# An attention loop on TensorE: small products and VectorE's side work take other places in the order

## The chip, the cores and the metric

The kernel runs on one core of one Trainium2 chip. A core has five engines that run their own instruction streams: TensorE (PE, matrix products; its weight loads are shown as PEld), VectorE (DVE), ScalarE (ACT), GpSimd (POOL) and SyncE (SP, used here for DMA queues and marks). The metric is the device time of one execution in microseconds (us), lower is better. A kernel is run several times and the median is given. A profile is one more execution, with its own time.

## What is computed

There are B = 16 graphs' inputs x of N = 1024 nodes and C = 64 channels, and one N x N matrix adj. All is in 32-bit floats. Layer 0 is an attention whose softmax goes over axis 1 and whose result passes through adj; layer 1 adds a two-hop graph convolution with adj. Each layer is followed by a residual sum and a layer norm.

```python
Q = jnp.einsum('bnc,oc->bno', x, Wq) + bq
K = jnp.einsum('bnc,oc->bno', x, Wk) + bk
V = jnp.einsum('bnc,oc->bno', x, Wv)
score = jnp.einsum('bnc,bmc->bnm', Q, K)
score = jax.nn.softmax(score, axis=1)
score = jnp.einsum('bnm,mc->bnc', score, adj)
x = _layernorm(x + jnp.einsum('bnm,bmc->bnc', score, V))
...
x_stack = [x0]
for support in (adj, adj):
    x1 = jnp.einsum('ij,bjk->bik', support, x0)
    x_stack += [x1, 2.0 * jnp.einsum('ij,bjk->bik', support, x1) - x0]
x = _layernorm(x + concatenate(x_stack) @ weight + bias)
```

## The kernel before

The kernel reorders the attention: it computes y = adj x for all batches first (so score times adj never exists as an N x N product), and then per batch the softmaxed scores times y, and that times Wv. Products with adj are done by a seven-product scheme over the four quadrants of adj ("hops": `hop_0` and `hop_1` make adj x for batches 0 to 7 and 8 to 15, `hop_z` starts layer 1). Each of the seven products of a hop has a number n; product n needs a sum of quadrants on the adj side (`sums_of_adj`) and one on the other side (`Hop.sums`), made by VectorE.

Batches go in pairs: p = 0 to 7 is the pair, j = 0 or 1 the batch in it. Batch j's channels lie on partitions 0-63 (j = 0) or 64-127 (j = 1). Nearly every product of the attention loop has a 64x64 stationary tile, so the array is used as four quarters: the row half is set by the partitions that are read, the column half by the partitions that are written. "Upper" below is the row half of partitions 0-63, "lower" that of 64-127. A product in 32-bit floats is two matmul instructions on the chip.

The loop runs over steps (p, m), m = 0 to 7 being a block of 128 of the softmax rows. One step makes the scores of the next block, `nxt`, and uses up the exponentials of this one. In TensorE's order a step is, with the row half in brackets:

1. `scores(sc, nxt, 0, h)` for h = 0, 1 [upper], with the end of the last step's run between them (`tail.part(1, 1)` [lower])
2. `weighted(before, 1, h)` [lower]: us times the exponentials of the last block, second half, accumulated into `acc`
3. the first part of a run, `todo[0].part(0, 0)` [upper]. A run is a 128 x 256 piece of one hop product; 69 of them are taken one or two a step from the list `runs`
4. `scores(sc1, nxt, 1, 0)` [lower]; then, in some steps, the small product of j = 0 [upper]; then `scores(sc1, nxt, 1, 1)` [lower], `todo[0].part(0, 1)` [upper]
5. `weighted(p, m, 0, 0)` [upper], the small product of j = 1 [lower], `weighted(p, m, 0, 1)` [upper], `todo[-1].part(1, 0)` [lower]

The small products are: `values` of pair p-1 in step (p, 1) (16 products of 64 columns per batch), `project` of pair p+1 in step (p, 4) (2 of 512 columns per batch, makes `GT`), and `mix` of an earlier pair in steps (p, 7), (p, 0), (p, 2), (p, 3) (4 of 192 columns per batch). Both of a step, j = 0 and then j = 1, are written into the same PSUM bank, the one of two (`f0`, `f1`) that the step's run doesn't use, so the second waits until the first is evicted. Each has an eviction for ScalarE (`by_scalar`) and one for VectorE (`by_vector`).

The softmax of a block is `exps` (line 384 on): VectorE takes the negated maximum of a row (`nm`, L393), ScalarE the exponential with its row sum (`e`, L395). `sc` and `sc1` are two PSUM tiles of two banks each, so the scores of one block can start only when the exponential of the last has read its tile. In the next step `scaled` makes `ri` = 1/sum (L402) and `us` = y times `ri` (L404), without which `weighted` cannot start.

VectorE's stream in a step is: eviction of the last step's run, `ri`, `us`, first maximum, `by_vector` of the first small product, what `first_gap` holds for this step, second maximum, `by_vector` of the second small product, (with two runs) the eviction of the first run, what `second_gap` holds. The two dictionaries are filled by `at(...)` by hand: hop sums, weight preparation (`value_weights`, `mix_weights`), and for each pair `means`, `centre`, `spread`, `normed`, and the transposes (`transposed`, `x0T`), which VectorE does blockwise and POOL's DMA queue finishes by way of DRAM (one write, four reads). `attended` copies `acc` to `oT` on ScalarE at m = 0; it must be read before the next pair's `weighted` can open `acc` again. SP's queue in the loop carries only marks that keep products of the two row halves into one bank in order. The order of each engine's stream is the order of the program (`manual_schedule`).

Of the kernel before, what the change touches and what calls it, by code (L numbers as in the profile page):

```python
# [9 lines left out]
FP = mybir.dt.float32  # L10
# [16 lines left out]
def gnn_kernel(  # L27
# [13 lines left out]
    nc = tc.nc  # L41
# [112 lines left out]
    def mix_weights():  # L154
        nc.vector.tensor_add(w24, w1s[:, 2], w1s[:, 4])
        nc.vector.tensor_scalar(w3[:, 0], w24, 2.0, None, op0=ALU.mult)
        nc.vector.tensor_add(w3[:, 1], w1s[:, 1], w1s[:, 3])
        nc.vector.tensor_sub(w3[:, 2], w1s[:, 0], w24)
        for j in range(2):
            nc.vector.tensor_add(w3[half[j], 2], w3[half[j], 2], ident[half[j], half[j]])  # L160
        centred(w3)

# [178 lines left out]
    def project(p, js, pq):  # L341


        if 0 in js:
            GT[p] = att.tile([P, N], FP, tag="GT", name="GT")
        for b in range(2):
            for j, t in zip(js, pq):
                nc.tensor.matmul(  # L348
                    t[half[b]], g2[half[j], half[j]], xT(p)[half[j], ts(b, H)], start=True, stop=True
                )  # L350

        def places():
            for j, t in zip(js, pq):
                for b in range(2):
                    g = by_block(GT[p])[half[j], 2 * b : 2 * b + 2]
                    yield j, g, t[half[b]].rearrange("c (a k n) -> c a k n", a=2, k=K8), gb[half[b]]

        def by_scalar():
            for j, g, q, bias_ in places():
                if j == 0:  # L360
                    nc.scalar.activation(g, q, AF.Identity, bias=bias_)  # L361

        def by_vector():
            for j, g, q, bias_ in places():
                if j == 1:
                    nc.vector.tensor_scalar(g, q, bias_, None, op0=ALU.add)
        return by_scalar, by_vector

    def means(p):
        XM[p] = small.tile([P, G], FP, tag="xm", name="xm", bufs=NP)  # L370
        nc.vector.tensor_reduce(XM[p], rows(p), AX.X, ALU.add)
        nc.vector.tensor_scalar(XM[p], XM[p], 1.0 / C, None, op0=ALU.mult)

    def centre(p):
        nc.vector.tensor_tensor(
            rows(p), rows(p), XM[p][:, :, None].to_broadcast([P, G, C]), ALU.subtract
        )
# [48 lines left out]

    def attended(p):
        OT[p] = att.tile([P, N], FP, tag="oT", name="oT", bufs=1)
        nc.scalar.activation(by_block(OT[p]), by_place(ACC.pop(p)), AF.Copy)

    def values(p, js, po):


        for k in range(K8):
            for t in range(2):
                for j, o in zip(js, po):
                    n = k * P + t * C
                    nc.tensor.matmul(  # L438
                        o[half[t], ts(k, C)], OT[p][half[j], n : n + C], wv2[half[j], half[j]],
                        start=True, stop=True,  # L440
                    )

        def by_vector():
            for j, o in zip(js, po):
                r = xs[:, p, :, half[j]]
                nc.vector.tensor_add(r, o.rearrange("p (k c) -> p k c", c=C), r)
        return (lambda: None), by_vector

# [31 lines left out]
    def mix(p, kk, js, pm):  # L480


        pm = [t.rearrange("p (s k c) -> p s k c", s=4, k=2) for t in pm]
        for k in range(2):
            for c in range(2):
                for j, t in zip(js, pm):
                    n = (kk + k) * P + c * C
                    nc.tensor.matmul(  # L488
                        t[half[c], 0:3, k], X0T[p][half[j], n : n + C], w3[half[j]],
                        start=True, stop=True,  # L490
                    )

# [8 lines left out]
        def by_vector():  # L501
            for j, t in zip(js, pm):
# [3 lines left out]
                )  # L506
        return by_scalar, by_vector

    def both(what, *args, banks=None):

        return what(*args, (0, 1), banks or [f_tile(f"both{j}") for j in range(2)])

# [71 lines left out]
    for hop, orders in (  # L584
        (hop_0, (((6, 7), ONE), ((5, 3), ONE))),
        (hop_1, (((1, 2), ONE), ((6, 7, 4), ONE), ((5, 3), ONE))),
        (hop_z, (((1, 2), ONE), ((3,), ONE), ((5,), ONE), ((6, 7, 4), ONE))),
    ):
        runs += [(hop, n, g) for order, groups in orders for g in groups for n in order]
# [9 lines left out]
    at(first_gap, (0, 2), sums_of_adj, 4)  # L599
    at(second_gap, (0, 3), value_weights)  # L600
    at(second_gap, (0, 5), mix_weights)
    for step, n in ((1, 0), 1), ((1, 1), 2), ((1, 6), 4), ((2, 1), 3):
        at(second_gap, step, hop_1.sums, n)
    for step, n in ((HP + 1, 1), 1), ((HP + 2, 0), 2), ((HP + 2, 1), 3), ((HP + 2, 5), 4):
        at(second_gap, step, hop_z.sums, n)
    for p in range(NP):
        at(second_gap, (p, 5 if p != HP + 2 else 6), means, p)
        if p in (HP + 1, NP - 1):
            at(second_gap, (p, 6), centre, p)
        else:  # L610
            at(first_gap, (p + 1, 0), centre, p)
        if p + 1 < NP:
            at(second_gap, (p + 1, 2), spread, p)
            at(second_gap, (p + 1, 3), normed, p)
            at(first_gap, (p + 1, 4), x0T, p)
        if p + 2 < NP:
            at(second_gap, (p, 7), lambda p: transposed(p, xT(p)), p + 2)

# [45 lines left out]
    for p in range(NP):  # L664
        q = p - 1
        for m in range(K8):
# [9 lines left out]
            if before:  # L676
                weighted(*before, 1, 0)
            scaled(p, m)
            for evict in late:
# [5 lines left out]
            if before:  # L685
                weighted(*before, 1, 1)
                if m == 0:
                    attended(q)
                PU.pop(before)
            todo[0].part(0, 0)  # L690
            what = small_of.get((p, m))
            sc1 = sc_tile("sc1")
            scores(sc1, *nxt, 1, 0)
            if what:
                by_scalar, by_vector = what[0](*what[1:], (0,), [f_other("small0")])
                by_scalar()
            else:
                todo[0].part(0, 1)
# [37 lines left out]
    for h in range(2):  # L736
        for j in range(2):
# [4 lines left out]
            if sum_mark:  # L742
                behind_mark([made], sum_mark.pop())
    attended(NP - 1)
    evict()
# [417 lines left out]
```

## Time and profile before

| what | us |
|---|---|
| median of 3 runs (lowest to highest) | 582.25 (582.12 to 582.33) |
| the profiled execution, device time | 582.28 |
| its span in the profile | 580.5 |
| PE busy | 565.7 (97%) |
| PEld busy | 405.8 (70%) |
| DVE busy | 442.5 (76%) |
| ACT busy | 244.6 (42%) |
| POOL busy | 153.0 (26%) |
| first maximum of step (0,0) to that of step (7,6) | 37.67 to 417.88 |

Times of the trace are counted from the span's start; 1.8 us of the device time lie around the span. A line of a timeline gives the start, how long the piece took, engine, source line, operation, out<-in, partitions x elements and the count of merged instructions, and in brackets how long the engine had been idle and what released it. A group's line gives its count, busy time, the mean of one in ns, and the idle time ahead of it. A busy PE means that at least one matmul is under way; the four quarters of the array are not told apart. The clock granted to TensorE was 0.994 of full speed over the span.

### The profile page before, as it was taken

How to read it: one execution, taken by the hardware profiler on the slowest of the kernel's cores; microseconds unless marked ns; L12 is line 12 of the kernel's file. 1: busy time of each engine (PE TensorE's matmuls, PEld its weight loads, DVE VectorE, ACT ScalarE, POOL GpSimd, SP SyncE). 2: the span in 40 equal slices, each digit the busy share in tenths (PEclk: the TensorE clock that was granted, in tenths of full speed). 3: DMA queues.
4: the chain of work that ended last, by engine and by line, in shares of the span. 5: the costliest groups of instructions: out<-in, count | busy, mean ns of one | idle time of the engine just before them, and what ended most of it. 6: DMA issues, size and time to landing. Idle time of an engine off the chain costs nothing.

```text
span 580.5 us, 14496 instructions
## 1 busy us (share of the span) xinstructions
PE 565.7 (97%) x6150; PEld 405.8 (70%) x6150; DVE 442.5 (76%) x725; ACT 244.6 (42%) x517; POOL 153.0 (26%) x145
## 2 busy tenths in 40 slices
PE   9999999999999999999999999999999999999992
PEld 8757647567756766766676776677668789888652
DVE  0789788878877788787788778888847475799784
ACT  1133544545456455553554455455431300041561
POOL 0001001211211120121121012102102795693784
PEclk9999999999999999999999999999999999999997
DMA  8902002012022020101202010100201400001943
GB/s 262 333 5 71 2 2 75 37 38 76 1 73 74 3 73 23 53 37 39 75 1 75 14 62 32 44 2 2 75 1 43 103 1 2 1 17 44 204 144 100
DMA packets 20994, 33.66 MB, mean 58 GB/s; under 512 B 3010, under 2 KB 12482, under 8 KB 20546
## 3 DMA queue, kind: packets, MB, share of 16 engines
q0 software_dynamic: 6880, 18.88, 11.2%
q1 hardware_dynamic: 14050, 13.86, 7.3%
q8 instruction: 48, 0.79, 0.6%
q14 instruction: 16, 0.13, 0.1%
HBM read 16.48 MB, written 12.06 MB: 49 GB/s over the span
## 4 chain that ended last, share of the span: by engine, by line
PE 91%; DVE 3%; ACT 2%; issue 2%; DMA 0%; POOL 0%; SPq 0%; POOLq 0%; ACTq 0%; DVEq 0%
PE p L267 21%; PE sc L382 18%; PE acc L416 17%; PE w L770 15%; PE w L1078 3%; PE small L488 3%; PE small L348 3%; PE pu L257 3%; PE wide L770 2%; PE small L438 2%; PE pv L257 1%; PE p L257 1%; PE both L488 1%; ACT GT L361 1%; DVE nm L393 1%
## 5 line engine op out<-in xcount | busy, mean ns | idle before, releaser
L382 PE MATMUL sc<-xT,GT 64*64 64x512 f32 x1024 | 242.1, 592 | 0.7 <-ACT e L395 0.5
L416 PE MATMUL acc<-e,us 64*64 64x512 f32 x1008 | 242.0, 592 | 0.2 <-DVE us L404 0.2
L395 ACT ACTIVATE e<-sc,nm 128x1024 f32<-128x1024 f32 x128 | 142.7, 1115 | 118.2 <-DVE nm L393 117.9
L393 DVE TENSOR_REDUCE nm<-sc 128x1 f32<-128x1024 f32 x128 | 156.0, 1220 | 22.2 <-PE sc L382 21.2
L456 POOL TENSOR_TENSOR rstd<-var,expo 128x16 f32<-128x16 f32 (+3 forms) x21 | 50.9, 2428 | 145.4 <-DVE var L454 145.3
L416 PEld LDWEIGHTS acc<-e,us 64*64 64x64 f32 x1008 | 69.8, 133 | 27.4 <-issue 12.3
L382 PEld LDWEIGHTS sc<-xT,GT 64*64 64x64 f32 x1024 | 69.4, 132 | 13.3 <-issue 6.2
L334 POOL DMA_DIRECT2D d<-blocks x14 | 8.4, 596 | 200.2 <-DVE blocks L329 200.2
L267 PE MATMUL p<-XB,S 64*64 64x256 f32 x480 | 59.2, 378 | 0.0
L267 PE MATMUL p<-UY,aT 64*64 64x256 f32 x480 | 59.0, 377 | 0.0
L267 PE MATMUL p<-UY,S 64*64 64x256 f32 x384 | 46.2, 376 | 0.0
L267 PE MATMUL p<-XB,aT 64*64 64x256 f32 x352 | 42.8, 377 | 0.0
L267 PEld LDWEIGHTS p<-XB,S 64*64 64x64 f32 x480 | 33.7, 133 | 12.7 <-issue 4.5
L267 PEld LDWEIGHTS p<-UY,aT 64*64 64x64 f32 x480 | 33.9, 133 | 11.5 <-issue 2.8
L488 PE MATMUL small<-w,x0T_k 64*64 64x192 f32 x384 | 40.7, 329 | 0.0
L488 PEld LDWEIGHTS small<-w,x0T_k 64*64 64x64 f32 x384 | 25.1, 132 | 14.3 <-DVE xs L503 11.3
L267 PEld LDWEIGHTS p<-UY,S 64*64 64x64 f32 x384 | 27.1, 133 | 9.8 <-issue 2.9
L498 ACT ACTIVATE UY<-small 128x128 f32<-128x128 f32 x48 | 13.3, 277 | 46.5 <-PE small L488 46.5
L267 PE MATMUL p<-xs,aT 64*64 64x256 f32 x256 | 31.5, 377 | 0.0
L267 PEld LDWEIGHTS p<-XB,aT 64*64 64x64 f32 x352 | 24.8, 133 | 9.5 <-issue 3.3
L267 PE MATMUL p<-xs,S 64*64 64x256 f32 x256 | 30.9, 376 | 0.0
L503 DVE TENSOR_TENSOR xs<-small,bias 128x128 f32<-128x128 f32 x48 | 14.0, 291 | 22.0 <-ACT XB L499 21.9
(211 smaller groups left out, 941.0 us busy)
## 6 DMA issues: line engine op xcount, KB each, us to landing
d<-blocks POOLq DMA_DIRECT2D x14, 512.0 KB, 2.9
xs<-own POOLq DMA_DIRECT2D x8, 512.0 KB, 6.5
xT<-d POOLq DMA_DIRECT2D x28, 128.0 KB, 3.3
x0T<-d POOLq DMA_DIRECT2D x28, 128.0 KB, 2.9
out_dram<-xs SPq DMA_DIRECT2D x14, 256.0 KB, 2.2
xs<-in_x_dram SPq DMA_DIRECT2D x3, 1024.0 KB, 7.2
aT<-in_adjT_dram SPq DMA_DIRECT2D x8, 256.0 KB, 5.2
aT<-in_adjT_dram SPq DMA_DIRECT2D x4, 512.0 KB, 8.2
```

The costliest lines, as they stand in the source:

```text
L257: nc.tensor.matmul(po[t * w : (t + 1) * w], SIDE[n][:, k, j : j + w], self.side[n][:, :, k, :], start=start, stop=True, skip_group_check=True,
L267: nc.tensor.matmul(po[half[c]], SIDE[n][half[t], k, i * P + c * C : i * P + (c + 1) * C], self.side[n][half[t], :, k, :], start=t == 0 and ...
L348: nc.tensor.matmul(t[half[b]], g2[half[j], half[j]], xT(p)[half[j], ts(b, H)], start=True, stop=True)
L382: nc.tensor.matmul(sc[half[c], ts(h, H)], GT[p][half[j], m * P + c * C : m * P + (c + 1) * C], xT(p)[half[j], ts(h, H)], start=True, stop= ...
L393: nc.vector.tensor_reduce(nm, sc, AX.X, ALU.max, negate=True)
L395: nc.scalar.activation(e, sc, AF.Exp, bias=nm, accum_out=sm[:, j : j + 1])
L416: nc.tensor.matmul(ACC[p][half[j], ts(h, H)], us[half[t], j], es[j][half[t], ts(h, H)], start=m == 0 and t == 0, stop=m == K8 - 1, skip_gr ...
L456: nc.gpsimd.tensor_tensor(rstd, var, expo[:, 0:n], ALU.pow)
L488: nc.tensor.matmul(t[half[c], 0:3, k], X0T[p][half[j], n : n + C], w3[half[j]], start=True, stop=True,)
L503: nc.vector.tensor_tensor(xs[:, p, kk : kk + 2, half[j]], t[:, 2], bias[:, None, :].to_broadcast([P, 2, C]), ALU.add,)
L770: nc.tensor.matmul(po[:, ts(g, b.shape[1] * P)], a[:, k, ts(g, P)], b[:, :, k, :], start=start and g == 0 and k == 0, stop=True, skip_grou ...
L1078: nc.tensor.matmul(po, SIDE[n][:, k, ts(i, P)], B_F[n][:, k, cols], start=k == 0, stop=k == K4 - 1)
```

## The change

The change leaves what is computed as it is and alters the order.

- Small products come as a list of parts (`made`), issued apart from their evictions. The first part of j = 0 is issued ahead of `scores(sc1, nxt, 1, 0)` and the other parts behind it; of j = 1, the first part where the product was, the others behind `weighted(p, m, 0, 1)`. Only `values` has two parts; `project` and `mix` have one.
- `project`'s evictions are split otherwise: of j = 0 one half goes to ScalarE and one to VectorE; of j = 1 both go to ScalarE. Before, ScalarE had both of j = 0 and VectorE both of j = 1.
- All entries of `second_gap` but the first transpose move to `first_gap`, many to another step; `mix_weights` loses its last operation, which becomes an entry of step (1, 0). `means` no longer scales by 1/C; `centre` does that in one `scalar_tensor_tensor`.
- `exps(nxt, 1, sc1)` stands behind the first run's eviction in steps with two runs.
- `attended` is done in two halves, the first behind `weighted(before, 1, 0)`.
- In the hops' orders, products 6, 7 and 4 (of `hop_1` and `hop_z`) run one after the other instead of interleaved, and the sums that they need are made later.

```diff
--- before.py
+++ after.py
@@ -158,7 +158,6 @@
         nc.vector.tensor_sub(w3[:, 2], w1s[:, 0], w24)
         for j in range(2):
             nc.vector.tensor_add(w3[half[j], 2], w3[half[j], 2], ident[half[j], half[j]])
-        centred(w3)
@@ -343,37 +342,43 @@
         if 0 in js:
             GT[p] = att.tile([P, N], FP, tag="GT", name="GT")
-        for b in range(2):
-            for j, t in zip(js, pq):
-                nc.tensor.matmul(
-                    t[half[b]], g2[half[j], half[j]], xT(p)[half[j], ts(b, H)], start=True, stop=True
-                )
-        def places():
+        def made():
+            for b in range(2):
+                for j, t in zip(js, pq):
+                    nc.tensor.matmul(
+                        t[half[b]], g2[half[j], half[j]], xT(p)[half[j], ts(b, H)],
+                        start=True, stop=True,
+                    )
+        def places(vector):
             for j, t in zip(js, pq):
                 for b in range(2):
-                    g = by_block(GT[p])[half[j], 2 * b : 2 * b + 2]
-                    yield j, g, t[half[b]].rearrange("c (a k n) -> c a k n", a=2, k=K8), gb[half[b]]
+                    if vector == ((j, b) == (0, 1) if len(js) == 1 else j == 1):
+                        g = by_block(GT[p])[half[j], 2 * b : 2 * b + 2]
+                        q = t[half[b]].rearrange("c (a k n) -> c a k n", a=2, k=K8)
+                        yield g, q, gb[half[b]]
         def by_scalar():
-            for j, g, q, bias_ in places():
-                if j == 0:
-                    nc.scalar.activation(g, q, AF.Identity, bias=bias_)
+            for g, q, bias_ in places(False):
+                nc.scalar.activation(g, q, AF.Identity, bias=bias_)
         def by_vector():
-            for j, g, q, bias_ in places():
-                if j == 1:
-                    nc.vector.tensor_scalar(g, q, bias_, None, op0=ALU.add)
-        return by_scalar, by_vector
+            for g, q, bias_ in places(True):
+                nc.vector.tensor_scalar(g, q, bias_, None, op0=ALU.add)
+        return (made,), by_scalar, by_vector
     def means(p):
         XM[p] = small.tile([P, G], FP, tag="xm", name="xm", bufs=NP)
         nc.vector.tensor_reduce(XM[p], rows(p), AX.X, ALU.add)
-        nc.vector.tensor_scalar(XM[p], XM[p], 1.0 / C, None, op0=ALU.mult)
     def centre(p):
-        nc.vector.tensor_tensor(
-            rows(p), rows(p), XM[p][:, :, None].to_broadcast([P, G, C]), ALU.subtract
+        nc.vector.scalar_tensor_tensor(
+            rows(p), XM[p][:, :, None].to_broadcast([P, G, C]), -1.0 / C, rows(p),
+            op0=ALU.mult, op1=ALU.add,
         )
     def scores(sc, p, m, j, h):
@@ -424,27 +429,32 @@
         if h == 1 and not (t and m == K8 - 1):
             sum_mark.append(passed(made))
-    def attended(p):
-        OT[p] = att.tile([P, N], FP, tag="oT", name="oT", bufs=1)
-        nc.scalar.activation(by_block(OT[p]), by_place(ACC.pop(p)), AF.Copy)
+    def attended(p, h):
+        if h == 0:
+            OT[p] = att.tile([P, N], FP, tag="oT", name="oT", bufs=1)
+        a = slice(2 * h, 2 * h + 2)
+        nc.scalar.activation(by_block(OT[p])[:, a], by_place(ACC[p])[:, a], AF.Copy)
     def values(p, js, po):
-        for k in range(K8):
-            for t in range(2):
-                for j, o in zip(js, po):
-                    n = k * P + t * C
-                    nc.tensor.matmul(
-                        o[half[t], ts(k, C)], OT[p][half[j], n : n + C], wv2[half[j], half[j]],
-                        start=True, stop=True,
-                    )
+        def made(ks):
+            for k in ks:
+                for t in range(2):
+                    for j, o in zip(js, po):
+                        n = k * P + t * C
+                        nc.tensor.matmul(
+                            o[half[t], ts(k, C)], OT[p][half[j], n : n + C], wv2[half[j], half[j]],
+                            start=True, stop=True,
+                        )
         def by_vector():
             for j, o in zip(js, po):
                 r = xs[:, p, :, half[j]]
                 nc.vector.tensor_add(r, o.rearrange("p (k c) -> p k c", c=C), r)
-        return (lambda: None), by_vector
+        parts = [lambda b=b: made(range(4 * b, 4 * b + 4)) for b in range(2)]
+        return parts, (lambda: None), by_vector
     def inv_std(sq, n):
@@ -481,14 +491,16 @@
-        for k in range(2):
-            for c in range(2):
...
+        def made():
+            for k in range(2):
+                for c in range(2):
...
@@ -504,11 +516,14 @@
                     xs[:, p, kk : kk + 2, half[j]], t[:, 2],
                     bias[:, None, :].to_broadcast([P, 2, C]), ALU.add,
                 )
-        return by_scalar, by_vector
+        return (made,), by_scalar, by_vector
     def both(what, *args, banks=None):
-        return what(*args, (0, 1), banks or [f_tile(f"both{j}") for j in range(2)])
+        parts, *evict = what(*args, (0, 1), banks or [f_tile(f"both{j}") for j in range(2)])
+        for do in parts:
+            do()
+        return tuple(evict)
     u = att.tile([P, K4, Q], FP, tag="u", name="u", bufs=1)
@@ -583,8 +598,8 @@
     runs = []
     for hop, orders in (
         (hop_0, (((6, 7), ONE), ((5, 3), ONE))),
-        (hop_1, (((1, 2), ONE), ((6, 7, 4), ONE), ((5, 3), ONE))),
-        (hop_z, (((1, 2), ONE), ((3,), ONE), ((5,), ONE), ((6, 7, 4), ONE))),
+        (hop_1, (((1, 2), ONE), ((6,), ONE), ((7,), ONE), ((4,), ONE), ((5, 3), ONE))),
+        (hop_z, (((1, 2), ONE), ((3,), ONE), ((5,), ONE), ((6,), ONE), ((7,), ONE), ((4,), ONE))),
     ):
         runs += [(hop, n, g) for order, groups in orders for g in groups for n in order]
     two_runs = {(0, 1), (0, 2), (1, 0), (HP, 5), (HP + 1, 5), (HP + 1, 6)}
@@ -597,24 +612,23 @@
     at(second_gap, (0, 0), lambda: transposed(1, xT(1)))
     at(first_gap, (0, 1), sums_of_adj, 1)
     at(first_gap, (0, 2), sums_of_adj, 4)
-    at(second_gap, (0, 3), value_weights)
-    at(second_gap, (0, 5), mix_weights)
-    for step, n in ((1, 0), 1), ((1, 1), 2), ((1, 6), 4), ((2, 1), 3):
-        at(second_gap, step, hop_1.sums, n)
-    for step, n in ((HP + 1, 1), 1), ((HP + 2, 0), 2), ((HP + 2, 1), 3), ((HP + 2, 5), 4):
-        at(second_gap, step, hop_z.sums, n)
+    at(first_gap, (0, 3), mix_weights)
+    at(first_gap, (0, 4), value_weights)
+    for step, n in ((1, 0), 1), ((2, 0), 2), ((2, 5), 3), ((3, 0), 4):
+        at(first_gap, step, hop_1.sums, n)
+    at(first_gap, (1, 0), centred, w3)
+    for step, n in ((HP + 1, 5), 1), ((HP + 2, 0), 2), ((HP + 2, 7), 3), ((NP - 1, 0), 4):
+        at(first_gap, step, hop_z.sums, n)
     for p in range(NP):
-        at(second_gap, (p, 5 if p != HP + 2 else 6), means, p)
-        if p in (HP + 1, NP - 1):
-            at(second_gap, (p, 6), centre, p)
-        else:
-            at(first_gap, (p + 1, 0), centre, p)
+        at(first_gap, {2: (2, 1), 6: (4, 5)}.get(p, (p, 5)), means, p)
+        at(first_gap, {6: (5, 6)}.get(p, (p, 6)), centre, p)
         if p + 1 < NP:
-            at(second_gap, (p + 1, 2), spread, p)
-            at(second_gap, (p + 1, 3), normed, p)
+            at(first_gap, (p + 1, 2), spread, p)
+            at(first_gap, (p + 1, 3), normed, p)
             at(first_gap, (p + 1, 4), x0T, p)
         if p + 2 < NP:
-            at(second_gap, (p, 7), lambda p: transposed(p, xT(p)), p + 2)
+            at(first_gap, (p, 7), lambda p: transposed(p, xT(p)), p + 2)
     small_of = {(p, 1): (values, p - 1) for p in range(1, NP)}
     small_of.update({(p, 4): (project, p + 1) for p in range(NP - 1)})
@@ -675,6 +689,8 @@
             scores(sc, *nxt, 0, 1)
             if before:
                 weighted(*before, 1, 0)
+                if m == 0:
+                    attended(q, 0)
             scaled(p, m)
             for evict in late:
                 evict()
@@ -685,14 +701,18 @@
             if before:
                 weighted(*before, 1, 1)
                 if m == 0:
-                    attended(q)
+                    attended(q, 1)
                 PU.pop(before)
             todo[0].part(0, 0)
             what = small_of.get((p, m))
             sc1 = sc_tile("sc1")
+            if what:
+                parts, by_scalar, by_vector = what[0](*what[1:], (0,), [f_other("small0")])
+                parts[0]()
             scores(sc1, *nxt, 1, 0)
             if what:
-                by_scalar, by_vector = what[0](*what[1:], (0,), [f_other("small0")])
+                for do in parts[1:]:
+                    do()
                 by_scalar()
             else:
                 todo[0].part(0, 1)
@@ -712,15 +732,19 @@
                 todo[0].part(1, 0)
             weighted(p, m, 0, 0)
             if what:
-                by_scalar, by_vector = what[0](*what[1:], (1,), [f_other("small1")])
+                parts, by_scalar, by_vector = what[0](*what[1:], (1,), [f_other("small1")])
+                parts[0]()
                 by_scalar()
-            exps(*nxt, 1, sc1)
-            if what:
-                by_vector()
             if len(todo) > 1:
                 todo[0].part(1, 1)
                 todo[0].evict()
             weighted(p, m, 0, 1)
+            if what:
+                for do in parts[1:]:
+                    do()
+            exps(*nxt, 1, sc1)
+            if what:
+                by_vector()
             todo[-1].part(1, 0)
             for do in second_gap.get((p, m), ()):
                 do()
@@ -741,7 +765,8 @@
             )
             if sum_mark:
                 behind_mark([made], sum_mark.pop())
-    attended(NP - 1)
+    for h in range(2):
+        attended(NP - 1, h)
     evict()
     assert not runs
```

More of the change, by code (lines that the diff above doesn't have):

```diff
@@ L483, in mix @@
         pm = [t.rearrange("p (s k c) -> p s k c", s=4, k=2) for t in pm]
-        for k in range(2):
-            for c in range(2):
[L486 to L491, printed above, removed]
+        def made():
+            for k in range(2):
+                for c in range(2):
+                    for j, t in zip(js, pm):
+                        n = (kk + k) * P + c * C
+                        nc.tensor.matmul(
+                            t[half[c], 0:3, k], X0T[p][half[j], n : n + C], w3[half[j]],
+                            start=True, stop=True,
+                        )
         def part(dst, j):
```

## The prediction

> **What bounds the kernel now.** I read the page first, for the chain that ended last and the busy times.
>
> ```profile
> PE 91%; DVE 3%; ACT 2%; issue 2%; DMA 0%; POOL 0%; SPq 0%; POOLq 0%; ACTq 0%; DVEq 0%
> ...
> L393 DVE TENSOR_REDUCE nm<-sc 128x1 f32<-128x1024 f32 x128 | 156.0, 1220 | 22.2 <-PE sc L382 21.2
> ```
>
> TensorE is the bound, and VectorE has slack: 22.2 us of its idle time lies ahead of the maxima, waiting for scores. But TensorE's busy time hides its own loss. Every product here has a 64x64 stationary tile, so four fit in the array; a "busy" TensorE may have a half of it empty. So I took the matmuls of the attention loop by form, from the first maximum of step (0,0), 37.67 us, to that of step (7,6), 417.88 us.
>
> ```profile
> L416 PE MATMUL acc<-e,us 64*64 64x512 f32 x992 | 238.2, 592 | 0.2 <-DVE us L404 0.2
> L382 PE MATMUL sc<-xT,GT 64*64 64x512 f32 x996 | 237.5, 592 | 0.7 <-ACT e L395 0.5
> L488 PE MATMUL small<-w,x0T_k 64*64 64x192 f32 x384 | 40.7, 329 | 0.0
> L438 PE MATMUL small<-wv,oT 64*64 64x64 f32 x448 | 19.7, 222 | 0.1
> L348 PE MATMUL small<-xT,g 64*64 64x512 f32 x56 | 14.9, 604 | 1.7 <-ACT GT L361 1.7
> ```
>
> The timeline shows what one occupies: 512-column products of one row half start every 0.43 us (scores at 153.15, 153.58, 154.01, 154.44), those with 256 columns every 0.215, with 192 every 0.16, with 64 every 0.058. So the loop holds 2044 x 0.43 + 2192 x 0.215 (the products of L267) + 384 x 0.16 + 448 x 0.058 = 1438 us for one quarter of the array, 359 us for all four. The stretch lasts 380.2. About 21 us of it is an array partly empty: the ceiling of any reordering. A step without small product fills 12 slots of 0.43 = 5.16 us; with mix 5.80, with project 6.02, with values 6.09, with two runs 6.88.
>
> Then where it is empty, from timelines of one step per kind. Step (3,4), project:
>
> ```profile
> 207.48 0.62 PE L348 MATMUL small<-xT,g 64*64 64x512 f32 x2
> ...
> 208.08 0.59 PE L382 MATMUL sc<-xT,GT 64*64 64x512 f32 x2
> ...
> 208.94 0.60 PE L382 MATMUL sc<-xT,GT 64*64 64x512 f32 x2
> 209.21 0.62 PE L416 MATMUL acc<-e,us 64*64 64x512 f32 x2
> 210.19 0.65 PE L348 MATMUL small<-xT,g 64*64 64x512 f32 x2 [0.36 <-ACT GT L361]
> ```
> ```profile
> 208.76 1.38 ACT L361 ACTIVATE GT<-small,gb 64x512 f32<-64x512 f32 x2 [2.76 <-PE small L348]
> 210.16 1.11 ACT L395 ACTIVATE e<-sc,nm 128x1024 f32<-128x1024 f32 x1
> ```
>
> The first small product is through at 208.10, yet its eviction starts at 208.76, just after the scores that precede it in program order (208.08 + 0.59 = 208.67). The second small product uses the same bank and waits for both evictions, to 210.19. The lower row half is empty from 209.37, the upper from 209.64: (0.82 + 0.56)/2 = 0.69 us. The exponential behind the evictions is late too, and the next scores wait for it (0.32 us of one half, 0.16). Together 0.85.
>
> Step (3,1), values:
>
> ```profile
> 188.37 0.57 PE L438 MATMUL small<-wv,oT 64*64 64x64 f32 x14
> ...
> 189.21 0.60 PE L382 MATMUL sc<-xT,GT 64*64 64x512 f32 x2
> 189.22 0.88 PE L438 MATMUL small<-wv,oT 64*64 64x64 f32 x7
> 189.85 0.65 PE L382 MATMUL sc<-xT,GT 64*64 64x512 f32 x2
> ```
>
> Sixteen of the 32 small instructions run at full rate ahead of the scores they follow in program order; the rest limps, and stops for 0.43 us. Upper half: done at 188.32 + 16 x 0.058 = 189.25 if unbroken, next product at 189.88, 0.63 lost; lower half: 189.64 to 189.85, 0.21. Mean 0.42; the second small product costs 0.09 (bank) and 0.12 (the acc behind it at 191.91, due 191.68). Together 0.63.
>
> A mix step, (2,3): scores end 154.87, second small product at 155.11, once the bank is evicted: 0.24 of one half, 0.12; in steps (p,0), where the copy of acc comes first, (0.29 + 0.15)/2 = 0.22. Steps (0,5), (0,6): seven small VectorE operations and a mean between the second maximum and the next `ri`, 1.0 and 1.1 us.
>
> Sum: project 7 x 0.85 less 0.5 for the first two = 5.5; values 7 x 0.63 = 4.4; mix 18 x 0.12 + 6 x 0.22 = 3.5; pair 0 2.1; the other 5.5 is scattered.
>
> [...]
>
> **The change, part by part.**
>
> *Small product j=0 ahead of scores (1,0).* Same matmuls, same row halves in the same order, so no TensorE work is added. Its end is signalled before the scores': project eviction at 208.19 for 208.76. Half now goes to VectorE (0.75; its first maximum ends about 208.1), so both are done by 208.95 instead of 210.15, before the lower half is free (209.37): the 0.69 goes, and the exponential starts about 1.1 us earlier, so the 0.16 goes. Next late is ScalarE in the second half: both evictions of j=1 (2 x 0.69, before on VectorE) now stand ahead of the second exponential. The second scores leave the lower half at 209.37, the small product at 210.23 (signalled about 210.4), evictions to 211.8, exponential to 213.1; the next scores into its bank are due after the run's part (211.09) and six slots more, at 213.7. It fits by 0.6; I leave 0.15 per step. Gain 5.5 - 7 x 0.15 = 4.4.
>
> *Values in two parts.* If eight pairs on each side of the scores keep the queue moving, the 0.42 and the 0.12 go; nothing in the trace shows this order, so bounds 0 and 0.63, a loss excluded since no wait is added. I take 0.45: 3.2.
>
> *Mix.* Evictions come 0.5 us earlier (154.29 follows scores ending 154.18; the product ends about 153.7), more than the 0.24. The copy of acc is halved, the first half a 0.43 slot earlier; two of some 0.6 for one of 1.04 (estimate from that row and the 0.28 of 128 columns) is 0.2 us of ScalarE, 42% busy. Gain 3.0 of 3.5. After the loop the split copy costs at most 0.2, beside other products.
>
> *Weights of pair 0* move to (0,3) and (0,4), 1.7 and 0.9 us; their DMAs were issued by 17.8 with about 7 us to landing. Gain 1.8 of 2.1.
>
> *VectorE work ahead of the second maximum.* It used to lie under the second exponential (1.3 us); now it lengthens the chain first maximum, this work, second maximum, exponential, `ri`, `us`, next first maximum. Without work it takes 4.1 us (step (0,6): 76.48, e read out at 80.13, plus 0.45). With it, in us: (p,5) and (p,6) 5.3 each (1.21, 1.22), (p,7) 5.6 (transpose 1.24 and mix eviction), (p,0) 5.5 with a sum, (p,1) 4.7, (p,2) 5.7, (p,3) 5.5, (p,4) 6.0: 43.6 for a pair, TensorE 45.6. Only (p,5) and (p,6) exceed their 5.16, by 0.15; with a late first exponential after project I charge 0.3 per pair: +2.5 for eight. In two-run steps the first run's eviction also goes ahead of the second maximum and waits for products ending 14 slots = 6.0 us into a 6.88 us step; the eviction ends near 6.5, the maximum near 7.8, the exponential near 9.1, its bank is due at 6.88 + 6 x 0.43 = 9.4. Nothing charged; at most 0.5 x 6 = 3.
>
> *The rest.* The transpose's five POOL DMAs issue some 2 us earlier, on a queue that mostly waits for VectorE (200.2 us), past nothing but idleness; the power step on POOL (2.4 us) moves with its sum and still has a whole step before `normed`. SP's queue carries only marks in the loop. Dropping the scaling of the means saves 8 x 0.175 on VectorE, hidden; the fused centring should cost what the plain one does (0.36 for 192 elements, between 0.29 for 128 and 0.42 for 256 of a tensor_tensor). The hop orders regroup the same products; the sums still precede them by three steps or more.
>
> Sum: -4.4 - 3.2 - 3.0 - 1.8 + 2.5 = -9.9. Against this execution's 582.28 us: 572.4. The median, 582.25, is the same.
>
> **The rivals.** *Half given back.* The chain through both maxima leaves only 2.0 us per pair. If hand-overs that I didn't count cost 0.35 us a step, the chain reaches 46.4 and TensorE waits 0.8 a pair, 6.4 in all in place of my 2.5: 582.3 - 12.4 + 6.4 = 576. For it: mix steps now carry 1.4 us ahead of the second maximum. Against: 22 us of VectorE's idle time lies just there.
>
> *Slower.* The same second maximum, late in every step: bank sc1 stays held, TensorE stands at the next scores (1,0). A pair takes 48.1 us now ((2,5) at 165.72 to (3,5) at 213.78); this decides once the chain exceeds my 43.6 by 0.56 us a step. At 0.65, a pair is 48.8 and eight add 5.6: 588.
>
> *It does nothing.* Completion might not come earlier and the queue might break elsewhere, with the losses only moved: 582, within 0.2% (1.2 us, about what a measurement tells from no change).
>
> **How the numbers follow.** Forecast 0.64 (own range 567 to 575: values fully regained and no new wait give 568.7, and some of the scattered 5.5 may go too; values not at all give 575.6), half given back 0.21, no change 0.05, slower 0.10. Faster 0.85, same 0.05, slower 0.10. The range runs from 566 to 580.
>
> **What would show it.** Right: project evictions starting within 0.15 us of their small product's end, no wait of the second small product for GT; the values stop of 0.43 gone; pairs of about 47 us. Wrong: `sc` waiting for `e` in many steps, the second maximum later than 3 us after the first in plain steps, pairs at 48 or more.

## The result and the profile after

The changed kernel takes 578.79 us (median of 4 runs, 578.60 to 579.03) against 582.25: a ratio of 0.9941, 95% interval 0.9924 to 0.9958. It is faster by 3.5 us where 9.9 were forecast. Its profiled span is 576.8 us, before 580.5; the granted clock is 0.993, before 0.994.

The page of the changed kernel: first the chain that ended last, by engine; then groups of instructions (count, busy us, mean ns of one, idle time ahead and what ended it).

```profile
PE 85%; DVE 6%; ACT 3%; DMA 2%; issue 1%; SPq 0%; POOL 0%; POOLq 0%; ACTq 0%; DVEq 0%
...
L421 PE MATMUL acc<-e,us 64*64 64x512 f32 x1008 | 240.1, 591 | 5.3 <-ACT oT L437 5.3
...
L398 DVE TENSOR_REDUCE nm<-sc 128x1 f32<-128x1024 f32 x128 | 155.8, 1217 | 3.4 <-PE sc L387 3.0
```

Three readings. The chain runs through TensorE for 85% of the span, no longer 91%. The maxima wait for scores 3.0 us in all where it was 21.2. VectorE's idle time has not gone with that (it is 76% busy in both kernels); much of it has moved behind the exponential: `ri` now waits for `e` 17.8 us in all, where it was 3.9. And there is a wait that the kernel before hardly had: all of TensorE stands 5.3 us, ahead of `acc` products, for ScalarE's `oT` (L437), the copy of `acc`.

The view of waits (what waited, for what; us in total, times, longest us) of the changed kernel, and then of the kernel before:

```profile
DVE ri L407 <- ACT e L400: 17.8, 33, 1.3
...
PEld acc L421 <- ACT oT L437: 11.5, 7, 1.7
...
PE acc L421 <- ACT oT L437: 5.3, 7, 0.8
...
PEld small L349 <- DVE GT L370: 5.1, 7, 0.7
...
PEld small L500 <- DVE xs L515: 2.3, 12, 0.2
```
```profile
PEld small L488 <- DVE xs L503: 11.3, 24, 0.8
...
PEld small L348 <- ACT GT L361: 7.6, 7, 1.3
...
DVE ri L402 <- ACT e L395: 3.9, 7, 1.3
...
PEld acc L416 <- ACT oT L429: 2.1, 6, 0.3
```

The waits for the bank between two `mix` products (L488, now L500) fell from 11.3 to 2.3 us. That of `project`'s second product (L348, now L349) fell only from 7.6 to 5.1. The new wait, that of `acc` for `oT`, occurs seven times, once for each of the first seven pairs, in step (p+1,0). This is one of them, step (3,0), in the timeline of the changed kernel (start, duration, engine, line, operation; in brackets the idle time and its releaser):

```profile
179.99 0.60 PE L421 MATMUL acc<-e,us 64*64 64x512 f32 x2
...
181.34 0.65 PE L421 MATMUL acc<-e,us 64*64 64x512 f32 x2 [0.76 <-ACT oT L437]
181.35 0.65 PE L266 MATMUL p<-XB,aT 64*64 64x256 f32 x4
```
```profile
180.69 0.60 ACT L437 ACTIVATE oT<-acc 128x512 f32<-128x512 f32 x1
```

`weighted(before, 1, 0)` is the product at 179.99. The next, `weighted(before, 1, 1)`, writes the other half of `acc`, yet starts only when ScalarE has copied the first half, at 181.34. Ahead of the wait, products of the lower row half start 0.43 us apart (179.56, 179.99), so by this rate it was free again at 179.99 + 0.43 = 180.42: 0.92 us empty. The upper half is empty too: its next product, which follows the waiting one in TensorE's order, starts at 181.35. If the other six are like this one, seven times 0.92 are 6.4 us, the size of the missing gain.

### The profile page after: what moved, and what is told of

Same layout as the page of the kernel before. It is cut to its first block, busy times and chain, and to the rows that moved or that the text cites. A ratio compares the mean times of both kernels' runs of the same rounds, so it can differ in the third digit from the quotient of the medians.

```text
span 576.8 us, 14499 instructions
## 1 busy us (share of the span) xinstructions
PE 558.9 (97%) x6150; PEld 398.2 (69%) x6150; DVE 438.2 (76%) x710; ACT 254.8 (44%) x532; POOL 153.0 (27%) x145
## 3 DMA queue, kind: packets, MB, share of 16 engines
q0 software_dynamic: 6880, 18.88, 11.3%
## 4 chain that ended last, share of the span: by engine, by line
PE 85%; DVE 6%; ACT 3%; DMA 2%; issue 1%; SPq 0%; POOL 0%; POOLq 0%; ACTq 0%; DVEq 0%
PE p L266 19%; PE sc L387 18%; PE acc L421 15%; PE w L795 14%; PE small L500 4%; PE w L1103 3%; PE wide L795 2%; DVE nm L398 2%; PE pu L256 2%; PE small L349 2%; PE small L447 2%; ACT e L400 2%; PE pv L256 1%; PE p L256 1%; DMA aT<-in_adjT_dram 1%
## 5 line engine op out<-in xcount | busy, mean ns | idle before, releaser
L421 PEld LDWEIGHTS acc<-e,us 64*64 64x64 f32 x1008 | 69.2, 133 | 36.4 <-ACT oT L437 11.5
L387 PEld LDWEIGHTS sc<-xT,GT 64*64 64x64 f32 x1024 | 66.7, 132 | 13.9 <-ACT e L400 5.5
L266 PE MATMUL p<-XB,aT 64*64 64x256 f32 x352 | 43.6, 378 | 0.0
L500 PE MATMUL small<-w,x0T_k 64*64 64x192 f32 x384 | 39.5, 323 | 0.0
L500 PEld LDWEIGHTS small<-w,x0T_k 64*64 64x64 f32 x384 | 26.5, 133 | 10.1 <-issue 3.5
L266 PEld LDWEIGHTS p<-UY,S 64*64 64x64 f32 x384 | 26.0, 133 | 10.2 <-issue 2.8
L808 ACT COPY own<-w 128x512 f32<-128x512 f32 x8 | 4.5, 587 | 54.6 <-PE w L795 54.6
```

What stands on the lines that cost most here:

```text
L266: nc.tensor.matmul(po[half[c]], SIDE[n][half[t], k, i * P + c * C : i * P + (c + 1) * C], self.side[n][half[t], :, k, :], start=t == 0 and ...
L387: nc.tensor.matmul(sc[half[c], ts(h, H)], GT[p][half[j], m * P + c * C : m * P + (c + 1) * C], xT(p)[half[j], ts(h, H)], start=True, stop= ...
L421: nc.tensor.matmul(ACC[p][half[j], ts(h, H)], us[half[t], j], es[j][half[t], ts(h, H)], start=m == 0 and t == 0, stop=m == K8 - 1, skip_gr ...
L500: nc.tensor.matmul(t[half[c], 0:3, k], X0T[p][half[j], n : n + C], w3[half[j]], start=True, stop=True,)
```

## The experiments

Each kernel was measured beside runs of the kernel before, whose medians were 582.24 to 582.41 us. "The loop" below is the stretch from the first maximum of step (0,0) to that of step (7,6) in the profiles: 380.2 us before, 375.5 in the changed kernel. Its end is a mark on VectorE, and that mark has moved against TensorE's work: from it to TensorE's first product behind the loop (L770 before, L795 in the changed kernel) it is 9.5 us in the kernel before (417.88 to 427.42) and 10.5 in the changed kernel (413.15 to 423.67) and in combined. So, beside the kernel before, the loop of a kernel with VectorE's moves looks about 1.0 us shorter than TensorE's work has become; among themselves these kernels compare.

**whole_copy**: the changed kernel with `acc` copied in one piece again.

```diff
                 weighted(*before, 1, 0)
-                if m == 0:
-                    attended(q, 0)
...
                 if m == 0:
-                    attended(q, 1)
+                    attended(q)
```

> The changed kernel with acc copied in one piece again, behind both of its last products. Theory 1 (the halved copy makes the products (before,1,1) of the steps (p,0) wait for ScalarE, 0.97 us in each of seven steps): 572.0 us, 571 to 573.5, and no hole of 1 us in (p,0). Theory 2 (the chain through both maxima is what is long, and the wait only sits on its slack): 577 to 579, with TensorE waiting for e in its place.

**split_alone**: the kernel before with nothing but the halved copy.

> The kernel before with nothing but the copy of acc in two halves. Theory 1: the same wait arises here, about 0.9 us in seven steps: 587 to 589.5. Theory 2: 582 to 583.5, since the exponential is early in this order and ScalarE free.

whole_copy took 572.05 us (571.44 to 572.42; ratio 0.9823, 0.9810 to 0.9837), split_alone 588.71 (588.39 to 589.15; 1.0111, 1.0097 to 1.0125). So the halved copy costs 6.7 us inside the change and 6.5 by itself. The waits of split_alone are those of the changed kernel:

```profile
PEld acc L416 <- ACT oT L431: 11.5, 7, 1.6
PE acc L416 <- ACT oT L431: 5.3, 7, 0.8
```

In whole_copy no wait of TensorE as a whole for `oT` is left, and of the weight loads' 11.5 us 1.3 are left (2.1 in the kernel before).

**two_tiles**: the copy stays halved, but `acc` is two PSUM tiles of one bank each instead of one tile of two banks (`pv` and `wide`, which use the same place outside the loop, likewise).

```diff
-            ACC[p] = pacc.tile([P, N], FP, tag="acc", name="acc")
+            ACC[p] = [pacc.tile([P, H], FP, tag=f"acc{i}", name=f"acc{i}") for i in range(2)]
...
-                ACC[p][half[j], ts(h, H)], us[half[t], j], es[j][half[t], ts(h, H)],
+                ACC[p][h][half[j]], us[half[t], j], es[j][half[t], ts(h, H)],
```

> The changed kernel with acc as two tiles of one bank each, copy still halved: no product of the second half can be held for the copy of the first. If the wait comes from the two halves being one tile: 570.5 to 572.5, at or below the run with the whole copy. If the copy of the first half really stands in the way of the products into the other bank: 578 to 579.5.

571.11 us (570.92 to 571.27; 0.9808, 0.9795 to 0.9821). Step (3,0) of two_tiles, TensorE and then ScalarE:

```profile
178.55 0.59 PE L421 MATMUL acc<-e,us 64*64 64x512 f32 x2
...
178.98 0.59 PE L421 MATMUL acc<-e,us 64*64 64x512 f32 x2
```
```profile
178.82 0.60 ACT L437 ACTIVATE oT<-acc 128x512 f32<-128x512 f32 x1
```

The products follow each other at 0.43 us, and ScalarE reads the first half from 178.82 to 179.42 while TensorE writes the second at 178.98. The copies and products are those of the changed kernel, and each half is again 128x512; what differs is that the halves are two tiles. So the wait came from the two halves being one tile in the program. Without it the halved copy is 0.9 us better than the whole one.

**small_alone**: the kernel before with the small products ahead of the scores, `values` in two parts and `project`'s evictions split. VectorE's other work, the hops' orders and the copy stay as before.

```diff
+            if what:
+                parts, by_scalar, by_vector = what[0](*what[1:], (0,), [f_other("small0")])
+                parts[0]()
             scores(sc1, *nxt, 1, 0)
             if what:
-                by_scalar, by_vector = what[0](*what[1:], (0,), [f_other("small0")])
+                for do in parts[1:]:
+                    do()
```

> The kernel before with only the small products moved ahead and in two parts, and project's evictions split as in the change; VectorE's other work and the copy of acc as before. By the terms of the prediction -4.4 -3.2 -3.0: 571.7. Taking from the trace of the changed kernel that the two project evictions of one bank run one after the other, 0.3 us a step is left: 573 to 575. Rival (the small products gain only because VectorE's work moved out of their way): above 578.

574.58 us (574.08 to 574.88; 0.9867, 0.9853 to 0.9880): a gain of 7.7.

**values_one**: whole_copy with `values` in one part, behind the first scores as before.

```diff
-        parts = [lambda b=b: made(range(4 * b, 4 * b + 4)) for b in range(2)]
+        parts = [lambda: made(range(K8))]
+        if js == (0,):
+            parts.insert(0, lambda: None)
```

> The run with the whole copy (572.05 us), values in one part and behind the scores again, as in the kernel before. The prediction's term says that two parts give 0.45 us in seven steps: 575.2 (574.3 to 576.3), with the stop of 0.43 us among the small products back. If the parts give nothing and only the earlier start of values did: 572 to 573.

576.14 us (575.92 to 576.43; 0.9890, 0.9874 to 0.9907), 4.1 more than whole_copy, or 0.58 per step. The stop can be seen in step (3,1), first of values_one, then of whole_copy:

```profile
186.85 0.59 PE L387 MATMUL sc<-xT,GT 64*64 64x512 f32 x2
186.87 0.88 PE L444 MATMUL small<-wv,oT 64*64 64x64 f32 x7
187.49 0.65 PE L387 MATMUL sc<-xT,GT 64*64 64x512 f32 x2
```
```profile
186.20 0.60 PE L387 MATMUL sc<-xT,GT 64*64 64x512 f32 x2
186.21 0.39 PE L444 MATMUL small<-wv,oT 64*64 64x64 f32 x7
...
186.62 0.60 PE L387 MATMUL sc<-xT,GT 64*64 64x512 f32 x2
```

In one part, seven small matmuls stretch over 0.88 us and the next scores come 0.64 us after those at 186.85; in two parts the seven take 0.39, and scores follow at 186.62, 0.42 after those at 186.20, the full rate. The edit undoes two things at once: it joins the parts, and it puts j = 0's small product behind the scores. All 32 in one go ahead of the scores were not tried, so how much of the 4.1 us the cut brings and how much the place isn't shown.

**project_evict**: whole_copy with `project`'s evictions where they were, both of j = 0 on ScalarE and both of j = 1 on VectorE; the product stays ahead of the scores.

```diff
-                    if vector == ((j, b) == (0, 1) if len(js) == 1 else j == 1):
+                    if vector == (j == 1):
```

> The run with the whole copy, project's evictions as before: both of j=0 on ScalarE, both of j=1 on VectorE. If the two evictions of one bank run one after the other anyway, the split between engines brings nothing for the second small product, and j=1 on VectorE frees the second exponential: 570.5 to 572.3. If they had overlapped as the prediction took it, taking the split away costs 0.3 to 0.6 us in seven steps: 574 to 576.

571.41 us (571.30 to 571.95; 0.9811, 0.9794 to 0.9827): 0.6 better than with the split, though the two ranges of single runs overlap (whole_copy 571.44 to 572.42).

**vector_alone**: the kernel before with VectorE's moves alone: the entries moved to `first_gap` and other steps, the hops' orders, the fused `centre` and the exponentials' place.

```diff
-            exps(*nxt, 1, sc1)
-            if what:
-                by_vector()
             if len(todo) > 1:
                 todo[0].part(1, 1)
                 todo[0].evict()
             weighted(p, m, 0, 1)
+            exps(*nxt, 1, sc1)
+            if what:
+                by_vector()
```

> The kernel before with VectorE's work moved, the hops regrouped and the means fused, as in the change; small products and project's evictions where they were, acc copied whole. The prediction's terms for it: -1.8 for the weights of pair 0 and +2.5 for the longer chain, so 583 (582 to 584). If its gain simply adds to that of the small products (574.58 with them alone, 572.05 with both): 579.7 (579 to 580.5).

581.22 us (580.89 to 583.49; 0.9984, 0.9976 to 0.9991): a gain of 1.1. Together with small_alone and split_alone this makes -7.7 - 1.1 + 6.5 = -2.3, and the whole change gives -3.5. Where the difference lies can be read from whole_copy, whose edits are those of small_alone and vector_alone together: it gains 10.2 where the two add to 8.8. So the small products and VectorE's moves help each other by about 1.4 us.

**maximum_first**: two_tiles with the second maximum ahead of the first run's eviction in steps with two runs, as it was before the change.

```diff
+            else:
+                exps(*nxt, 1, sc1)
             if len(todo) > 1:
                 todo[0].part(1, 1)
                 todo[0].evict()
```

> The run with acc as two tiles (571.11 us), the second maximum ahead of the first run's eviction in the six steps with two runs, as in the kernel before. The trace has TensorE waiting for e after two such steps (0.35 us in (0,3), 0.27 and 0.35 around (4,6)). If the late maximum makes these: 570.0 to 570.6. If the following chain makes them anyway: 570.8 to 571.5.

569.75 us (569.49 to 569.89; 0.9780, 0.9764 to 0.9796): 1.4 less than two_tiles. Step (4,5) has two runs. The timeline of the changed kernel there:

```profile
260.40 1.22 DVE L398 TENSOR_REDUCE nm<-sc 128x1 f32<-128x1024 f32 x1
...
264.87 1.21 DVE L398 TENSOR_REDUCE nm<-sc 128x1 f32<-128x1024 f32 x1
...
266.19 1.11 ACT L400 ACTIVATE e<-sc,nm 128x1024 f32<-128x1024 f32 x1 [3.25 <-DVE nm L398]
...
267.84 1.22 DVE L398 TENSOR_REDUCE nm<-sc 128x1 f32<-128x1024 f32 x1
```

From the second maximum to the next step's first it is 2.97 us: maximum, exponential, `ri`, `us`. The second maximum comes 4.47 after the first, so the step lasts 7.44. In maximum_first, where the products of this step are the same:

```profile
255.48 1.22 DVE L398 TENSOR_REDUCE nm<-sc 128x1 f32<-128x1024 f32 x1
...
258.87 1.21 DVE L398 TENSOR_REDUCE nm<-sc 128x1 f32<-128x1024 f32 x1
...
261.82 1.22 DVE L398 TENSOR_REDUCE nm<-sc 128x1 f32<-128x1024 f32 x1
```

The second maximum comes after 3.39, the remaining chain takes 2.95, and the step lasts 6.34. This distance between first maxima isn't the gain: over the six steps with two runs it falls from 43.6 us in two_tiles to 39.5, but the loop only from 367.8 to 366.3, since steps around them get longer.

**combined**: maximum_first with the edit of project_evict.

> maximum_first with project's evictions as before the change (both of j = 0 on ScalarE, both of j = 1 on VectorE); the small product still stands ahead of the scores. If the 0.6 us that the split of the evictions cost beside whole_copy come back here too: 569.75 - 0.6, about 569.1. If they were bound up with the late second maximum, which maximum_first has already mended: about 569.7.

567.94 us (567.84 to 568.08; 0.9749, 0.9736 to 0.9763), the fastest of all: 14.5 us under the kernel before, measured beside it (582.41). The gain over maximum_first, 1.8, is more than either value expected; 1.3 of it lies in the loop (366.27 to 364.94), the rest outside it, unexplained. Its chain, from the page:

```profile
PE 94%; DMA 1%; DVE 1%; ACT 1%; SPq 0%; POOL 0%; issue 0%; POOLq 0%; ACTq 0%
```

What the split of the evictions costs shows in the `project` step (3,4). First the changed kernel:

```profile
205.71 1.22 DVE L398 TENSOR_REDUCE nm<-sc 128x1 f32<-128x1024 f32 x1
206.22 0.62 PE L349 MATMUL small<-xT,g 64*64 64x512 f32 x2
206.89 0.68 ACT L366 ACTIVATE GT<-small,gb 64x512 f32<-64x512 f32 x1 [1.61 <-PE small L349]
...
207.60 0.76 DVE L370 TENSOR_SCALAR GT<-small,gb 64x512 f32<-64x512 f32 x1 [0.67 <-ACT GT L366]
...
208.41 0.65 PE L349 MATMUL small<-xT,g 64*64 64x512 f32 x2
...
209.67 1.23 DVE L398 TENSOR_REDUCE nm<-sc 128x1 f32<-128x1024 f32 x1
...
210.99 1.11 ACT L400 ACTIVATE e<-sc,nm 128x1024 f32<-128x1024 f32 x1
```

Then combined:

```profile
201.05 1.22 DVE L398 TENSOR_REDUCE nm<-sc 128x1 f32<-128x1024 f32 x1
...
201.56 0.62 PE L349 MATMUL small<-xT,g 64*64 64x512 f32 x2
...
202.22 1.38 ACT L366 ACTIVATE GT<-small,gb 64x512 f32<-64x512 f32 x2 [1.61 <-PE small L349]
...
203.64 1.22 DVE L398 TENSOR_REDUCE nm<-sc 128x1 f32<-128x1024 f32 x1 [0.22 <-PE sc L387]
203.66 0.65 PE L349 MATMUL small<-xT,g 64*64 64x512 f32 x2
...
204.96 1.11 ACT L400 ACTIVATE e<-sc,nm 128x1024 f32<-128x1024 f32 x1
```

In the changed kernel VectorE's eviction waits 0.67 us for ScalarE's, so the two stand one behind the other. From the first small product's last start to the second small product it is 2.19 us with the split and 2.10 without: nothing won. But VectorE's 0.67 and 0.76 lie ahead of the second maximum, which comes 3.96 after the first with the split and 2.59 without, and the second exponential is later by as much. (maximum_first, which differs from combined in the split alone, has the 3.96 too.) A `project` step, from first maximum to first maximum, lasts 6.81 us on average in the changed kernel, hardly less than the 6.84 of the kernel before, and 6.36 in combined.

**two_gt**: maximum_first with `GT` as two tiles, to see why VectorE waits there.

```diff
-            GT[p] = att.tile([P, N], FP, tag="GT", name="GT")
+            GT[p] = [att.tile([P, H], FP, tag=f"GT{b}", name=f"GT{b}", bufs=2) for b in range(2)]
...
-                        g = by_block(GT[p])[half[j], 2 * b : 2 * b + 2]
+                        g = GT[p][b][half[j]].rearrange("c (k a n) -> c a k n", k=K8, a=2)
```

> maximum_first with GT as two tiles, one for each half that an eviction of project writes (blocks' columns 0-63 and 64-127), so that ScalarE's and VectorE's evictions of j = 0 share only the PSUM bank that they read. Theory A, the two wait for each other because they write one tile (their places in GT lie interleaved): VectorE's half starts with ScalarE's, both are done about 0.8 us after the small product, the second small product no longer waits, and with 0.1 to 0.3 us for each of seven steps the time is 568.0 to 569.2. Theory B, they wait because they read one PSUM bank: VectorE's half still starts some 0.7 us after ScalarE's, and the time is that of maximum_first, 569.75 within 0.3.

569.30 us (569.10 to 569.57; 0.9774, 0.9761 to 0.9787). The wait is still there, in the timeline of step (3,4):

```profile
202.87 0.68 ACT L366 ACTIVATE GT<-small,gb 64x512 f32<-64x512 f32 x1 [1.62 <-PE small L349]
...
203.59 0.76 DVE L370 TENSOR_SCALAR GT<-small,gb 64x512 f32<-64x512 f32 x1 [0.68 <-ACT GT L366]
```

So a common tile to write isn't its cause. The changed kernel's trace agrees: ahead of the loop, `project` of pair 0 is evicted from two banks into one `GT` tile, and there ScalarE (from 26.68, 1.39 us) and VectorE (from 26.73, 1.53 us) work side by side. What the evictions of step (3,4) still share is the PSUM bank that they read, theory B, and the PSUM tile in it; these two weren't told apart. The loop lasts 366.3 us as in maximum_first. The 0.45 us between the medians, more than the 0.3 allowed for theory B, lie outside the loop and stay unexplained.

## Why the prediction was right and wrong

It was right in direction, and wrong in size above all by one step. That step is the sentence on the copy of `acc`: halved, "0.2 us of ScalarE, 42% busy", and so at no cost. Only ScalarE's added time was priced. The halved copy also sits between two groups of TensorE's products into the same tile, a new wait on the engine that bounds the kernel (85% of the chain that ended last), and the other row half waits with it: in step (3,0) the held product starts at 181.34, the next of the upper half at 181.35. It cost 6.7 us (whole_copy, split_alone), and two_tiles showed that the tile, not the work, made the wait. The kernel without this piece takes 572.05 us, near the forecast of 572.4, but that is luck in part. The small products brought 7.7 us of the 10.6 forecast; VectorE's moves brought 1.1 where a loss of 0.7 was forecast, and the two together 1.4 that no term had:

| term | forecast | what the runs show |
|---|---|---|
| copy of `acc` halved | 0 | +6.7 in the change, +6.5 alone |
| `values` in two parts | -3.2 | -4.1 (values_one) |
| `project` and `mix` | -4.4 - 3.0 | -3.6 (small_alone's -7.7 less those 4.1, if `values` is worth as much there) |
| pair 0's weights, VectorE's chain | -1.8 + 2.5 | -1.1 (vector_alone) |
| small products and VectorE's moves together | 0 | -1.4 (whole_copy) |
| all | -9.9 | -3.5 |

- *Project.* The first half of the step held: the eviction starts at 206.89, within 0.05 us of its product's end (206.84), no longer behind the scores. "Both are done by 208.95" fails: that time counts from a first maximum at 206.97, which here starts at 205.71, so it means 207.69. The evictions end at 208.36, 0.67 us later, because VectorE's half waits for ScalarE's. The sentence that the wait of the second small product would go is wrong: 5.1 of 7.6 us remain. The chain of step (p,4), put at 6.0 us, took 6.8. The mark "no wait of the second small product for GT" decided this point against the forecast. That the split itself costs time is shown by combined, 1.8 us; the 0.6 of project_evict point the same way.
- *Values.* The stop of 0.43 is gone; in values_one 0.58 per step came back for the 0.45 taken. The bound of 0.63 held. That eight pairs on each side of the scores keep moving was the author's estimate from the sixteen small matmuls that ran ahead in step (3,1) of the kernel before (188.32 to 188.78, the scores ahead of them in the order starting at 188.78); what sets how many run ahead was not shown.
- *Mix.* The waits of L500 are nearly gone, as forecast. Its share in us wasn't measured by itself, so how the 3.8 missing of the joint 7.4 divide between `mix` and `project` stays open; the remaining waits speak for `project`.
- *VectorE's chain.* In plain steps its length was forecast well. Steps (p,5) and (p,6) without a second run last 5.21 to 5.32 us, step (7,5) for instance 5.21 with the second maximum 2.26 after the first, for a forecast of 5.3. In steps with two runs nothing was charged, because only the bank of `sc1` was followed. The chain through `ri` to the next first maximum is the one that ends too late: 4.47 + 2.97 = 7.44 in step (4,5), against the 6.88 that the forecast estimated for TensorE. The late maximum in these steps costs 1.4 us in all (maximum_first). The upper bound of 3 held. The net of all VectorE moves was a gain of 1.1, not a loss of 0.7.
- *Pairs.* (2,5) to (3,5) went from 48.1 to 47.7 us in the changed kernel, with the halved copy in it, and to 46.8 in whole_copy, where about 47 was the mark.

Of the rivals, "half given back" gave a time closer to the result, 576, but its mechanism isn't the cause: with VectorE's work left where the change puts it, whole_copy reaches 572. The copy was named by no rival.

## What to carry to other kernels

An operation that is cut in two and moved between an engine's writes to the same tile is not free because its engine has time (here 6.7 us, with ScalarE 42% busy before): ask which instruction of the bounding engine now stands behind it, and whether the two pieces are separate tiles (as two tiles the halved copy was 0.9 us better than the whole one). When work moves ahead of a step of a recurrence, follow the chain to the start of the next round (here through `ri` and `us`, 4.47 + 2.97 us in step (4,5)), not only to the buffer that comes free. An eviction shared between two engines is halved only if both run at the same time. In step (3,4) of the changed kernel, from one bank, VectorE's half starts at 207.60, when ScalarE's (206.89 to 207.57) is over; ahead of the loop, from two banks, the two start at 26.68 and 26.73.

## What was not expected of the hardware

- The two evictions of `project` for j = 0 read different partition halves of one bank, and still VectorE's waits for ScalarE's: 0.67 us in step (3,4) of the changed kernel, 0.68 in two_gt, where they write two tiles. Whether they can overlap in another program was not shown.
- The order of 64-column products matters at equal work: 32 small matmuls (two for each of 16 products) in one go behind the scores cost 0.58 us a step against two goes of 16, one on each side of them (values_one), and the scores of the other row half are held up with them (0.64 us from one to the next where it is 0.42).
- TensorE's busy share is 97% in both kernels and 98% in combined, while the loop before had, by the forecast's estimate (1438 us of single quarters in 380.2, so 3.8 of the four at work on average), about 21 us of empty array, and combined takes 14.3 us less from its first scores to the first product behind the loop (397.2 to 382.9).
